# First layer of a four-layer graph network: out-of-block edge rows skipped in every tile's gather instead of in the last two tiles of a block

## The chip, the cores and the metric

The kernel runs on one core of one Trainium2 chip. A core has a matrix engine (PE in the profile, with its weight loads as PEld), three engines for elementwise work (DVE, ACT, POOL), a queue engine (SP) and 16 DMA engines that they share. The metric is the device time of one launch in microseconds. The time of the kernel before the change is the median of ten runs, 3303.32 us, the runs lying between 3298.07 and 3307.70 us.

## The reference, cut to what matters

Four layers follow each other, each added to its input. Only the first is touched:

```
edge_index = stack([src, dst])                  # 106250 edges, sorted by dst, 6250 nodes
def L0_gnn(x, edge_index, edge_attr, W1, b1, W2, b2):
    row, col = edge_index
    h = concatenate([x[row], edge_attr], axis=1)      # 256 + 256 wide
    h = relu(h @ W1 + b1)
    agg = segment_sum(h, col, 6250)
    cnt = segment_sum(ones, col, 6250)
    agg = agg / maximum(cnt, 1)
    return relu(concatenate([x, agg], axis=1) @ W2 + b2)
x = x + L0_gnn(layernorm(x), ...)
x = x + L0_ffn(...)        # attention over 131072 other edges, then 4 experts
x = x + L1_gnn(...)        # second sum over the 106250 edges
x = x + L1_ffn(...)        # gated experts
```

So each edge needs the row of its source node, already multiplied by the upper half of W1 (the kernel calls this table `y_dram`), plus its own attributes times the lower half of W1; the rectified sum is added up by destination node.

## The kernel before, in words

**Blocks and windows.** The 6250 nodes are cut into 49 blocks of 128 (the last has 106). As the edges are sorted by destination, a block's edges are contiguous. For each block the kernel takes a window of 2304 edges, 18 tiles (`CW`) of 128, that starts at the block's first edge; the start is counted on the chip (`start`, L1086) and clamped so that the window stays inside the edge list. With 17 edges per node a block has some 2176 edges, so in most blocks the edges of the next block lie in the last two tiles, numbers 16 and 17. In the last block the clamp moves the start back, and edges of the block before it lie in the first tiles.

**Source numbers.** `load_windows` (L1189) prepares seven blocks at a time: it reads source and destination numbers, turns them on PE, clamps them (L1219 to L1221), marks in `inside` which edges belong to the block (L1231, L1232), and writes `src1` (L1241), the row numbers for the gathers. In between, at L1236 to L1240, the tiles from `SKIP` on get special treatment: 8192 (`FAR`) is added to the number of each edge that is not inside, so that the number is beyond the table. In the first group of seven blocks the first block is left out (`int(b == 0)`).

**Gathers.** The first layer runs over 147 groups of six tiles, three groups for each block (`groups1`, `RUNS`: group 0 has tiles 0, 1, 7, 8, 14, 15, group 1 has 2, 3, 9, 10, 16, 17, group 2 has 4, 5, 6, 11, 12, 13). `load_sources(q)` (L1603) issues on POOL one indirect DMA for each tile of group q, each of which fetches 128 rows of 1 KB from `y_dram` into one of four ring buffers `h` (L1581). The call itself is in the helper `gather`, L1184. For a tile from `SKIP` on, of any block but the first, the gather is issued with a bounds check: a row number beyond 6249 is no error, and no row is fetched for it. What is left in the buffer from earlier use is multiplied by zero later.

**What a group does besides.** In the loop at L1741, one pass for each group, `hidden(q)` multiplies the group's edge attributes by W1 on PE into `ph` (24 matmuls of 256 columns, recorded at the helper line L1170), `turn` transposes the attributes of the next group on DVE (L1613), `join(q)` adds `ph` to the gathered rows on DVE (L1631) and rectifies on ACT (L1632), and `add_up(q)` sums over destinations by matmuls with a 0/1 matrix (L1650). Preparation of later windows and a sort for the second layer are fed in between in small steps. The order on each engine is the program's (`ordered.pin()`, L1769).

**What holds a gather back.** In pass q the gathers of group q+2 are issued, after `add_up(q-2)`. With four buffers, group q+2 uses the buffer of group q-2, so the first gather of a group waits for the PE's sums of the group four before it. What holds a join back is the slower of two: the group's matmuls in `ph` and its six gathers.

After the first layer come the attention of the second layer with its first experts (gathers `sg`, 1280 to 2160 us) and the second sum over edges (gathers `hg`, 2212 to 3250 us). Their gathers are issued without the check.

The lines that matter:

```
SKIP, FAR = CW - 2, 8192.0                                               # L945
far = g[:, int(b == 0) :, SKIP:]                                         # L1236
V.scalar_tensor_tensor(
    far, flat3(inside)[:, int(b == 0) :, SKIP:], -FAR, far, op0=OP.mult, op1=OP.add
)
V.tensor_scalar(far, far, FAR, None, op0=OP.add)                         # L1240
gather(rows_of(q)[:, j, 0:D], y_dram, idx, w > 0 and t >= SKIP)          # L1608
```

Of the kernel before, what the change touches and what calls it, by code (L numbers as in the profile page):

```python
# [918 lines left out]
def kernel(ctx: ExitStack, tc: tile.TileContext, a: dict, out: bass.AP):  # L919
# [22 lines left out]
    C2 = E2 // P  # L942
    assert E2 % P == 0
    CW = 18
    SKIP, FAR = CW - 2, 8192.0  # L945
    WE = CW * P
    G = 8

# [1905 lines left out]
```

## Time and profile before

| what | value |
|---|---|
| median of ten runs | 3303.32 us |
| the profiled execution's own time | 3305.04 us |
| its span in the profile | 3303.2 us |
| mean granted PE clock over the span | 0.895 of full speed |
| first layer's gathers: number, first and last start | 882, at 99.6 and 1242.5 us |
| busy time from 100 to 1250 us: PE, DVE, ACT, POOL | 1104.6, 912.1, 321.8, 859.2 us |
| DMA engines, mean busy share in that stretch | 0.89 |

The profile shows one execution. Busy time is counted from instruction to instruction for each engine; the short spell in which an engine starts its next instruction is not counted, which matters for POOL here: a gather is recorded with about 0.95 us and the next begins about 0.30 us after its end. The profiled execution took 1.7 us more than the median, and 1.8 us of its time lie outside the span.

### The profile page before, as it was taken

The page shows a single profiled execution, that of the slowest core. Times are in us where ns is not written, and L with a number is a line of the kernel's source. Part 1 is how long each engine was busy: PE and PEld are TensorE (multiplying, and loading weights), DVE is VectorE, ACT ScalarE, POOL GpSimd, SP SyncE. Part 2 cuts the span into 40 slices and gives each one's busy share as a digit, 9 for nine tenths or more (in the row PEclk, how much of TensorE's full clock was granted, in tenths as well). Part 3 has the DMA queues.
Part 4 walks back from the last instruction along what each step waited for, and adds up shares of the span by engine and source line. Part 5 has one row for each costly group of instructions (what it writes and reads, how often), then busy time and mean ns, then how long its engine had stood idle before and what let it go on. Part 6 is the DMA issues. An engine that isn't in the chain of part 4 may idle for free.

```text
span 3303.2 us, 59987 instructions
## 1 busy us (share of the span) xinstructions
PE 2996.2 (91%) x18517; PEld 2355.9 (71%) x18517; DVE 2186.1 (66%) x6516; ACT 1184.2 (36%) x2200; POOL 2277.1 (69%) x2720
## 2 busy tenths in 40 slices
PE   6899999999999989999999999956788888889997
PEld 5667777777777767888888888844566666656775
DVE  6678887788777766878686869862344444444464
ACT  5122222222222323556666668740112112112234
POOL 1677777777777774777776677427777777777772
PEclk9999999999999999999999999965577777777798
DMA  6889898989999873445454545532222222222221
GB/s 180 193 192 197 200 208 192 199 195 207 205 208 202 197 175 101 111 111 136 102 153 104 140 97 153 130 102 53 53 59 59 59 59 59 60 60 60 60 66 30
DMA packets 704935, 423.34 MB, mean 128 GB/s; under 512 B 538699, under 2 KB 647303, under 8 KB 704604
## 3 DMA queue, kind: packets, MB, share of 16 engines
q1 hardware_dynamic: 422972, 201.12, 23.5%
q0 software_dynamic: 88512, 171.58, 23.1%
q10 hardware_dynamic: 193120, 46.69, 7.0%
q8 instruction: 150, 2.46, 0.3%
q14 instruction: 181, 1.48, 0.2%
HBM read 382.75 MB, written 42.50 MB: 129 GB/s over the span
## 4 chain that ended last, share of the span: by engine, by line
PE 52%; POOL 16%; issue 10%; DMA 10%; DVE 7%; ACT 2%; SPq 2%; ACTq 0%; DVEq 0%; POOLq 0%
PE ph L1170 28%; POOL hg L1184 14%; PE py L1170 10%; PE pe L1650 4%; PE pt L1170 3%; DMA ea<-in_edge_attr_dram 3%; DMA hg<-hp_dram,src 3%; PE pe L2714 2%; DMA h<-y_dram,src 2%; DMA rb<-low_dram 1%; POOL h L1184 1%; PE po L2032 1%; POOL sg L1184 1%; DVE et L1613 1%; DVE E L2010 1%
## 5 line engine op out<-in xcount | busy, mean ns | idle before, releaser
L1184 POOL DMA_INDIRECT h<-y_dram,src x882 | 859.6, 975 | 366.9 <-issue 204.1
L1184 POOL DMA_INDIRECT hg<-hp_dram,src x831 | 785.5, 945 | 280.7 <-issue 239.5
L1170 PE MATMUL ph<-w1b,et 128*128 128x256 f32 x3528 | 830.9, 387 | 13.6 <-DVE et L1613 8.1
L1184 POOL DMA_INDIRECT sg<-gat_dram,src x612 | 612.0, 1000 | 270.1 <-issue 167.2
L1170 PEld LDWEIGHTS ph<-w1b,et 128*128 128x128 f32 x3528 | 658.7, 191 | 161.5 <-issue 74.9
L2714 PEld LDWEIGHTS pe<-eq,hg 128*128 128x128 f32 x2036 | 396.5, 259 | 300.4 <-issue 151.9
L2714 PE MATMUL pe<-eq,hg 128*128 128x96 f32 (+15 forms) x2036 | 452.1, 352 | 153.8 <-DMA hg<-hp_dram,src 134.9
L2691 DVE TENSOR_SCALAR eq<-px,dst,ew 128x96 f32<-128x96 f32 x831 | 262.2, 368 | 245.7 <-PE pe L2714 146.9
L1170 PE MATMUL py<-w,hh 128*128 128x256 f32 x1568 | 399.4, 393 | 13.2 <-ACT hh L1833 11.9
L1170 PE MATMUL ph<-b_all,w 128*128 128x256 f32 (+1 forms) x1600 | 402.1, 388 | 1.0 <-ACT hh L1833 1.0
L1632 ACT ACTIVATE h<-h 128x1536 f32<-128x1536 f32 x147 | 218.4, 1486 | 501.7 <-DMA ea<-in_edge_attr_dram 184.5
L1631 DVE TENSOR_TENSOR h<-ph,h 128x1536 f32<-128x1536 f32 x147 | 258.1, 1756 | 169.7 <-PE ph L1170 120.8
L1170 PEld LDWEIGHTS py<-w,hh 128*128 128x128 f32 x1568 | 282.1, 192 | 51.2 <-ACT hh L1833 17.0
L1170 PEld LDWEIGHTS ph<-b_all,w 128*128 128x128 f32 x1600 | 284.1, 192 | 30.9 <-ACT hh L1833 1.5
L1613 DVE STREAM_TRANSPOSE et<-ea 128x1536 f32<-128x1536 f32 x147 | 260.7, 1773 | 14.6 <-DMA ea<-in_edge_attr_dram 10.1
L1833 ACT ACTIVATE hh<-ph,b 128x256 f32<-128x256 f32 (+1 forms) x400 | 166.9, 466 | 125.4 <-PE ph L1170 105.7
L2010 DVE TENSOR_SCALAR E<-nodes,bits 128x256 bf16<-128x256 bf16 (+5 forms) x612 | 187.5, 345 | 36.3 <-PE po L2032 35.5
L1650 PE MATMUL pe<-h,eq 128*32 128x257 f32 x2496 | 181.2, 395 | 0.0
L1833 ACT ACT_TABLE_LOAD x102 | 130.9, 1283 | 24.3 <-PE ph L1170 14.3
L1165 ACT ACTIVATE b_all<-pt 128x256 f32<-128x256 f32 x147 | 54.1, 377 | 217.5 <-PE pt L1164 214.1
L1170 PE MATMUL py<-ew,g 65*128 65x256 f32 x392 | 126.0, 449 | 1.0 <-DVE miss L2799 1.0
L1650 PEld LDWEIGHTS pe<-h,eq 128*32 128x32 f32 x2496 | 72.7, 111 | 69.7 <-issue 34.1
(358 smaller groups left out, 3930.8 us busy)
## 6 DMA issues: line engine op xcount, KB each, us to landing
ea<-in_edge_attr_dram SPq DMA_DIRECT2D x784, 64.0 KB
ea<-in_edge_attr_dram ACTq DMA_DIRECT2D x392, 64.0 KB
w<-in_L_ffn_W_dram SPq DMA_DIRECT2D x48, 512.0 KB
y<-ys SPq DMA_DIRECT2D x96, 256.0 KB
rb<-low_dram SPq DMA_DIRECT2D x84, 256.0 KB
ea<-in_edge_attr_dram ACTq DMA_DIRECT2D x196, 96.0 KB
ea<-in_edge_attr_dram SPq DMA_DIRECT2D x196, 96.0 KB
h<-y_dram,src POOLq DMA_INDIRECT x882
```

Of the source, the lines that this page charges most:

```text
L1165: SC.activation(dst, pt.rearrange("p c k -> p (c k)"), AF.Copy)
L1170: TE.matmul(dst, lhs(c), rhs(c), start=c == 0, stop=c == n - 1)
L1184: GP.indirect_dma_start(out=dst, out_offset=None, in_=table[0:NP, :], in_offset=IndirectOffsetOnAxis(ap=idx, axis=0), **more,)
L1613: V.transpose(et[q].rearrange("p c m k -> p m c k"), ahead.pop(q).rearrange("p m (c k) -> p m c k", c=2),)
L1631: V.tensor_add(h, ph.pop(q), h)
L1632: SC.activation(h, h, AF.Relu)
L1650: TE.matmul(sums[w][b * Q : (b + 1) * Q, :], some[:, (b - lo) * Q : (b - lo + 1) * Q], rows_of(q)[:, j, 0:WS], start=(g, b, j) in begin, s ...
L1833: SC.activation(hidden[u][:, f, :n, :], ph[:, f - f0, :n, :], AF.Gelu, bias=b1[:, e, f : f + 1],)
L2010: V.tensor_scalar(Es[g, j][:, 0:n, :].rearrange("p b k -> p (b k)"), nodes16[:, 0 : n * P], bits.bitcast(F32)[:, g * G + j : g * G + j + 1 ...
L2032: TE.matmul(pos[g][bank][:, to * HP : (to + 1) * HP], E[:, b - b0, :], pays[g % 2][:, j, :], start=bank not in begun, stop=bank not in lat ...
L2691: V.tensor_scalar(equals[k][:, j, :], lanes[:, 0:NW], dst_of[:, t : t + 1], ew[:, t : t + 1], op0=OP.is_equal, op1=OP.mult,)
L2714: TE.matmul(sums[b][:, lo - t0 * P : hi - t0 * P], hg[:, j, :], eq[:, j, lo - n0 : hi - n0], start=False, stop=after >= (t0 + n) * P,)
```

## The change

One constant:

```
-    SKIP, FAR = CW - 2, 8192.0
+    SKIP, FAR = 0, 8192.0
```

Two things follow from it. At L1236 to L1240 the two operations on row numbers now go over all 18 tiles of a block (126 elements per partition for seven blocks, 108 in the first group) instead of two tiles (14 and 12 elements). And at L1608 every gather of blocks 1 to 48 is issued with the bounds check: 864 of 882 gathers instead of 96. In the built program this adds one register write on POOL for each such gather, 864 in place of 96. On PE, ACT and SP the instructions, their order and their waits are the same as before; on POOL only those register writes are new; on DVE the two operations are wider, and in the preparation of the first seven blocks a few small operations change places. No transfer, buffer or wait is added or taken away elsewhere. Which edges count is decided by `dst1` and the 0/1 matrix, as before.

## The prediction

> **What bounds the kernel now.** The page first, for the engines; then busy time by stretch, for the stage that the change touches; then POOL's timeline, the waits of that stage and the chain of waits.
>
> ```profile
> POOL 1677777777777774777776677427777777777772
> L1184 POOL DMA_INDIRECT h<-y_dram,src x882 | 859.6, 975 | 366.9 <-issue 204.1
> ```
>
> The changed gathers are one group: 882 of them, 975 ns each, all in slices 2 to 15 of 40. POOL's "7" looks like slack, but busy time leaves out the start of each instruction. The busy time by stretch says the same of the stage alone (columns: us, then busy us and count of PE, PEld, DVE, ACT, POOL, granted PE clock, DMA share, GB/s):
>
> ```profile
> 100.00:1250.00 1150.00, 1104.60 (x6817) 857.95 (x6818) 912.07 (x1864) 321.76 (x534) 859.21 (x882) 0.98 0.89 198
> ```
>
> PE is busy 96%, POOL only 75%. POOL's timeline (start, duration, engine, idle before it) corrects that:
>
> ```profile
> 133.53 0.95 POOL L1184 DMA_INDIRECT h<-y_dram,src  x1 [0.30 <-issue]
> 134.78 1.01 POOL L1184 DMA_INDIRECT h<-y_dram,src  x1 [0.30 <-issue]
> 136.10 1.00 POOL L1184 DMA_INDIRECT h<-y_dram,src  x1 [0.30 <-PE ph L1170]
> 137.41 0.96 POOL L1184 DMA_INDIRECT h<-y_dram,src  x1 [0.30 <-issue]
> 138.69 0.96 POOL L1184 DMA_INDIRECT h<-y_dram,src  x1 [0.31 <-issue]
> 139.95 0.95 POOL L1184 DMA_INDIRECT h<-y_dram,src  x1 [0.30 <-issue]
> ```
>
> A gather every 1.25 us, with 0.30 us of start-up between any two. 882 times 1.25 is 1103 us, against 1143.9 us from the first gather's start (99.6) to the last one's end (1243.4). Going through the timeline for gaps above 0.305 us, I find 18, which hold 15.5 us more than that; the rest is gathers that last somewhat longer than 0.947 us. So POOL too works almost without a pause. Who paces whom is in the waits and the chain:
>
> ```profile
> DVE h L1631 <- PE ph L1170: 118.0, 74, 8.5
> DVE h L1631 <- DMA h<-y_dram,src: 35.5, 13, 5.3
> ```
> ```profile
> 325.34 3.65 PE ph L1170 x16
> 332.49 3.65 PE ph L1170 x16
> ...
> 1108.81 3.84 DMA h<-y_dram,src
> 1114.07 3.71 DMA h<-y_dram,src
> ```
>
> The join (L1631) waited 74 times for the matmuls, 13 times for the gathers: early on PE sets the pace and POOL runs up to the ring's limit; later the chain runs through the gathers. By the timeline, group 24 starts gathering at 284.8, group 84 at 755.5, group 132 at 1124.4 us: 7.85 us a group in the first stretch, 7.69 in the second, where POOL had one gap, of 0.2 us. PE's matmuls of groups 84 and 132 start at 768.0 and 1126.6: PE then needs only 7.47 us a group. The two engines are a few per cent apart, so what is added to POOL cannot be hidden for long.
>
> **The change part by part.** *The check.* It is in the trace: 96 gathers have it, tiles 16 and 17 of blocks 1 to 48. In the lines above they are the 1.01 and the 1.00. Over all 96 the median is 1.008 us and the shortest 1.003; the gathers of tiles 0 to 3 and 6 to 15 have 0.947 at every place in the group, and the shortest 0.941. The start-up before them is 0.305 us in both. Does the price come from skipped rows? Counting edges in the reference's sorted list, 25 of the 96 have no edge outside the block: median 1.008. For 24 all 128 are outside: 1.0085. It is a price of the form, 61 ns, whatever is skipped. The two gathers after each checked pair (0.96, tiles 4 and 5) last 0.960, 13 ns longer than others; why, the trace does not say.
>
> Newly checked are 16 tiles in 48 blocks, 768 gathers: 768 x 61 ns = 46.8 us. If the 13 ns is paid on coming back to unchecked gathers, it goes, since there is nothing to come back to: 96 x 13 ns = 1.2 us less. Sum 45.6 us of POOL's time. Bounds, since no run of checked gathers longer than two is in the trace: 0.995 us if 13 ns of the price belongs to changing between forms (16 x 48 ns less 4 x 13 ns a block: 34.4 us), 1.021 if both add up in a long run (18 x 1.021 us against 17.19 us a block: 56.8 us). I take 1.008, the measured one. The checked gathers' mean is 1.035, so 27 ns above their median, where the others' is 20 above (0.967); 7 ns x 768 = 5.4 us more at most, and I take half.
>
> *The register writes.*
>
> ```profile
> L1184 POOLq MOVE  x96: 29/29/35, 127.5 to 1229.2; - x96
> ```
>
> 768 more of 29 ns would be 22.3 us if POOL's start-up grew by them. It does not: the start-up before checked gathers is 0.305 us like before others, the second of a pair too, whose write falls into it. Counted at nothing; without that cover 22.3 us more.
>
> *The rows saved.* In blocks 1 to 47 no tile below 16 holds an edge from outside. Only the last block does, whose window is pushed back: 128, 128, 128 and 97 rows in tiles 0 to 3, 481 rows of 1 KB. At the stage's 198 GB/s that is 2.5 us of transfer, at the end of a stage whose joins wait there for PE (1232 to 1254 us). Counted at nothing; 2.5 us would be the most. This is the gain that the change has, and it covers one block in 49.
>
> *The wider DVE operations.* L1237 lasted 173 ns and L1240 174 ns at 14 elements. The same forms at 126 elements, L1232 and L1221, last 291 and 227. So 171 ns for seven blocks, 1.2 us over the seven preparations. The first lies at 63 us, 36 us ahead of the first gather; the others are spread in a stage where DVE is busy 912 of 1150 us. Nothing; if each delayed a join, 1.2 us.
>
> *What of it reaches the end.* POOL gains 45.6 us of work but loses waiting: it had 15.5 us of gaps, where the ring was full because PE was late. A POOL that is slower meets them with the ring less full. I carried the new durations through the 147 groups, holding the kernel's two rules (a group starts after the sums of the group four before; a join after the matmuls as timed and 2.4 us after its last gather, which is what the tightest ones show), and delaying PE two groups later by what a join is late. Gaps left: 2.1 us. POOL then ends 45.6 - 15.5 + 2.1 = 32.2 us later, the last join 30.9 us later, since before it came 11 us after its gather and now 9.7. With 7 ns more a gather the last join moves by 35.9, so with half of it 33.4. By the paces: 45.6 us over 144 groups is 0.32 a group, so POOL needs 7.69 + 0.32 = 8.00, above PE's 7.85 and 7.47.
>
> What is late next: the order on PE is fixed, so experts of the second layer cannot fill PE's new pauses. The write of `gat_dram` at 1276 us hangs on the last block's sums, and the second layer's gathers on it (1279.7); PE is busy 913 of 960 us after that. Nothing there waits for a clock of its own, so I pass the shift on whole: 3303.2 + 33 = 3336 us of span, 3338 with the 1.8 us outside; against the median, 1.7 us below that execution, 3336.3. Forecast **3336 us**.
>
> **Two rules weighed.** The Trainium skill, "DMA: Bandwidth & Descriptors", section "Issuing engines are not separate DMA queues", says that the time to initiate a DMA is usually small beside the transfer. Here it is not: 1.25 us of POOL for 128 KB, which at 198 GB/s are 0.66 us. By the rule only the saved rows would count and the sum would be 3301 us; by the row it is 3336. The other speaks against the change: "TensorE: Matmul & The Clock Gate", section "HAM oscillation — how this bites in real kernels", wants no pause of PE above some 3.4 us, or its clock halves. The stage has seven stretches at half clock of 3.4 to 6.8 us between 105 and 1243 us and a granted mean of 0.98. I see pauses of half a microsecond a group coming, and by the rule add nothing; one more half-clock stretch of 6.8 us would cost PE 3.4 us, which it has to spare.
>
> **The rivals.** *PE goes on setting the pace; no change.* For it: 74 waits against 13, PE 96% busy. Against: the paces. It would hold only if a gather cost less than (7.85 - 7.69) / 6 = 27 ns more; the 96 rows show 61. Time 3301 to 3306. Chance 0.05, a little of it for a price that a long run of checked gathers does not pay. *Faster: changing between the forms is all that costs.* The place is POOL, the price the 96 x (61 + 13) ns = 7.1 us that it then no longer pays, decisive if a checked gather in a long run lasts 0.947 or less: at most 3303 - 7 = 3296, where POOL is the bound. Against it: the second of each pair costs as much as the first. Chance 0.02. *A smaller price, 0.995 us.* The same working gives 21 us: 3324. Chance 0.15. *A larger one:* 1.021 us with all of the 7 ns gives 46.5 us, 3350; and if the register writes showed too, up to 3372. Chance 0.13. *PE loses its clock in this stage as in the last, where it waits for gathers at a granted 0.73:* 1105 x 0.98 / 0.73 = 1483 us of PE work, over 300 us more. Against: PE would pause 7% of the time here, in short pieces. Chance 0.02. The forecast itself, 3329 to 3343, has 0.63.
>
> **Range and chances.** Leaving out the faster and unchanged cases and the far end, 3319 to 3352: from 5 us under the small price to 2 us over the larger. Within 0.2% (6.6 us) a measurement cannot tell from no change. Faster 0.02, same 0.05, slower 0.93.
>
> **What would show it.** The changed profile should have gathers `h` of about 1.01 us median in blocks 1 to 48, start-up still 0.30, last start near 1275 us; joins that wait more often for the gathers than for `ph`; PE's busy time in the stage unchanged and the stage longer; gathers `sg` and `hg` as before, shifted. I am wrong if the long run's median is 0.95, or the start-up grows by 29 ns, or POOL's gaps stay at 15 us, or the second layer takes up the delay.

## The result, and the profile after

The changed kernel takes 3324.9 us (median of 8 runs, 3322.95 to 3327.19); the kernel before, run beside it, 3302.46 us (median of 28). The ratio is 1.0068, with a 95% interval of 1.0059 to 1.0077: 22.4 us slower. The profiled execution took 3321.77 us, 3.1 us less than the median, and the one of before 2.6 us more than its median of 28; so the two spans differ by 16.8 us only (3320.0 against 3303.2), and stages are compared here rather than spans.

The page of the changed kernel, costliest groups (count | busy us, mean ns | idle before):

```profile
L1184 POOL DMA_INDIRECT h<-y_dram,src x882 | 896.9, 1017 | 353.1 <-issue 195.3
L1184 POOL DMA_INDIRECT hg<-hp_dram,src x831 | 784.9, 945 | 280.6 <-issue 238.3
```

The first layer's gathers have 37.3 us more busy time than before (859.6), and their mean rose from 975 to 1017 ns; the last stage's gathers `hg` have the mean that they had. POOL's timeline of the changed kernel, in the stretch shown of before (start, duration, engine, idle before it):

```profile
131.91 1.00 POOL L1184 DMA_INDIRECT h<-y_dram,src  x1 [0.30 <-issue]
133.21 1.00 POOL L1184 DMA_INDIRECT h<-y_dram,src  x1 [0.30 <-issue]
134.51 1.00 POOL L1184 DMA_INDIRECT h<-y_dram,src  x1 [0.30 <-issue]
135.82 0.99 POOL L1184 DMA_INDIRECT h<-y_dram,src  x1 [0.30 <-issue]
```

Before, two gathers of 18 were longer than the others; now all have the same 1.00 us, with the same start-up. The line view of the gathers in the first layer (count: shortest/median/longest ns, first and last start):

```profile
L1184 POOL DMA_INDIRECT h<-y_dram,src x882: 942/998/1458, 99.8 to 1267.0; - x177
```
```profile
L1184 POOLq MOVE  x864: 29/29/35, 114.3 to 1261.5; - x173
```

The median is 998 ns, not 947 and not 1008. The last gather starts at 1267.0 us instead of 1242.5. There are 768 more register writes, and the start-up has not moved. Busy time of the stage to 1270 us (PE, PEld, DVE, ACT, POOL, granted clock, DMA share, GB/s) and the join's waits (us, times, longest):

```profile
100.00:1270.00 1170.00, 1107.56 (x6799) 855.62 (x6800) 911.40 (x1862) 319.60 (x530) 896.70 (x882) 0.98 0.87 193
```
```profile
DVE h L1631 <- DMA h<-y_dram,src: 81.0, 32, 7.9
DVE h L1631 <- PE ph L1170: 79.2, 43, 8.4
```

PE has the work that it had (1107.6 us in a stretch 20 us longer, 1104.6 before) at the same granted clock. The join waited 32 times for gathers, 13 before, and 43 times for the matmuls, 74 before: POOL has taken over part of the pace. By the timeline, POOL's gaps beyond 0.305 us shrank from 15.8 to 2.9 us (every excess counted; the 15.5 us of the prediction are the 18 clear gaps alone). The first gather of the second layer starts at 1303.6 instead of 1279.7 us; from there to the end it is 2016 us, 2024 before, so nothing is lost later, and the other profiles below lie between 2012 and 2024 for that part whatever they do in the first layer, but for the kernels that change the last stage and the four runs with pauses told of below.

### The profile page after: what moved, and what is told of

Its sections match the earlier page's. It is cut to its first block, busy times and chain, and to the rows that moved or that the text cites. A ratio compares the mean times of both kernels' runs of the same rounds, so it can differ in the third digit from the quotient of the medians.

```text
span 3320.0 us, 60755 instructions
## 1 busy us (share of the span) xinstructions
PE 3003.3 (90%) x18517; PEld 2353.9 (71%) x18517; DVE 2183.2 (66%) x6516; ACT 1183.3 (36%) x2200; POOL 2313.4 (70%) x2720
## 3 DMA queue, kind: packets, MB, share of 16 engines
q0 software_dynamic: 88512, 171.09, 22.7%
## 4 chain that ended last, share of the span: by engine, by line
PE 47%; POOL 15%; DMA 14%; issue 11%; DVE 8%; SPq 2%; ACT 2%; ACTq 0%; DVEq 0%; POOLq 0%
PE ph L1170 24%; POOL hg L1184 12%; PE py L1170 10%; DMA ea<-in_edge_attr_dram 6%; PE pe L1650 3%; PE pe L2714 3%; PE pt L1170 3%; DMA hg<-hp_dram,src 3%; DVE et L1613 2%; DMA h<-y_dram,src 1%; POOL sg L1184 1%; PE po L2032 1%; POOL h L1184 1%; DMA rb<-low_dram 1%; DVE E L2010 1%
## 5 line engine op out<-in xcount | busy, mean ns | idle before, releaser
L1184 POOL DMA_INDIRECT h<-y_dram,src x882 | 896.9, 1017 | 353.1 <-issue 195.3
L1613 DVE STREAM_TRANSPOSE et<-ea 128x1536 f32<-128x1536 f32 x147 | 260.7, 1773 | 14.8 <-DMA ea<-in_edge_attr_dram 9.7
```

Of the source, the lines that this page charges most:

```text
L1184: GP.indirect_dma_start(out=dst, out_offset=None, in_=table[0:NP, :], in_offset=IndirectOffsetOnAxis(ap=idx, axis=0), **more,)
L1613: V.transpose(et[q].rearrange("p c m k -> p m c k"), ahead.pop(q).rearrange("p m (c k) -> p m c k", c=2),)
```

## The experiments

Theory F: a gather issued with the bounds check costs POOL a fixed time more, whatever it skips, and what of that exceeds POOL's gaps is in the time. Against it stood M (the marking, with skipped rows and wider DVE operations), D (the DMA engines as the bound) and P (another share of PE and POOL in the pace). Each time below is a median with the ratio to before in the same run.

**The check alone.** `e1_check_all`: the check on every gather of blocks 1 to 48, the marking as before.

```
-  gather(rows_of(q)[:, j, 0:D], y_dram, idx, w > 0 and t >= SKIP)
+  gather(rows_of(q)[:, j, 0:D], y_dram, idx, w > 0)
```

> Every gather of blocks 1 to 48 has the bounds check, but edges outside the block are marked only in tiles 16 and 17, as in the kernel before; so no further row is skipped and the DVE operations are as narrow as before. Theory F (the checked form itself costs POOL 51 ns a gather in a long run, whatever is skipped): gathers of 0.998 us at the median, last gather's end near 1267 us, time 22 us above before (3325). Theory M (the marking costs: skipped rows or wider DVE operations): gathers of 0.947 and 3303 us.

3321.16 us against 3298.70: ratio 1.0075 (1.0061 to 1.0089), 22.5 us. On its page the gathers' busy time is the changed kernel's but for 0.9 us:

```profile
L1184 POOL DMA_INDIRECT h<-y_dram,src x882 | 896.0, 1016 | 350.1 <-issue 193.4
```

The gathers' median is 998 ns at nearly every place in the block, the last one ends at 1264.2 us. The check alone, without a row more skipped or an element more on DVE, gives the whole change.

**The marking alone.** `e2_mark_all`: every tile is marked, the check stays in tiles 16 and 17, and in block 48, where the 481 other rows lie.

```
-  SKIP, FAR = CW - 2, 8192.0
+  SKIP, FAR = 0, 8192.0
-  gather(..., w > 0 and t >= SKIP)
+  gather(..., w == T - 1 or (w > 0 and t >= CW - 2))
```

> The other half alone: all 18 tiles are marked, as in the changed kernel, but the check is on in tiles 16 and 17 of blocks 1 to 47 and in all tiles of block 48, the only one where marked rows lie elsewhere. The same rows are skipped as in the changed kernel. Theory F: 16 more checked gathers, 0.8 us of POOL, which the gaps swallow: within 2 us of before. Theory M: the changed kernel's time, 3325 us.

3296.37 us against 3298.70: 0.9995 (0.9986 to 1.0003). The same line of this kernel is that of before, with 1.6 us more:

```profile
L1184 POOL DMA_INDIRECT h<-y_dram,src x882 | 861.2, 976 | 363.0 <-issue 206.2
```

The same rows are skipped as in the changed kernel and nothing is lost or measurably won. M is out.

**Runs of two, three and four.** `e3_from_tile9`:

```
-  SKIP, FAR = CW - 2, 8192.0
+  SKIP, FAR = 9, 8192.0
```

> SKIP = 9: nine tiles a block are checked, in runs of two, four and three, with unchecked ones between. If the first two gathers of a run cost 10 ns more than later ones and the two unchecked ones after it 13 ns (theory F with a price for changing form), durations are 1.008 twice, then 0.998, then 0.960 twice, then 0.947; POOL has 21.5 us more work, and carried through the groups with the ring's rule the last join moves 10 us: 3312 to 3314. Without a price for changing form: 0.998 and 0.947 throughout, 14.9 us of work, last join 5.5 us later: 3308. If the time followed POOL's work one for one, with no gaps to take some of it: 3324.

3308.12 us against 3298.70: 1.0034 (1.0022 to 1.0045), 9.4 us. POOL's timeline of this kernel, tiles 0, 1, 7, 8 and 14 of one block:

```profile
310.72 0.96 POOL L1184 DMA_INDIRECT h<-y_dram,src  x1 [0.30 <-issue]
311.98 0.96 POOL L1184 DMA_INDIRECT h<-y_dram,src  x1 [0.30 <-issue]
313.24 0.95 POOL L1184 DMA_INDIRECT h<-y_dram,src  x1 [0.30 <-issue]
314.49 0.94 POOL L1184 DMA_INDIRECT h<-y_dram,src  x1 [0.30 <-issue]
315.74 1.01 POOL L1184 DMA_INDIRECT h<-y_dram,src  x1 [0.30 <-issue]
```

Two unchecked gathers after a checked run at 0.96, two at 0.95 and 0.94, then the first of the next run at 1.01. The medians over blocks 1 to 48, tile by tile in the order of issue (ns, the checked ones starred):

```
tile   0   1   7   8   14*   15*   2   3   9*    10*   16*  17*   4   5   6   11*   12*   13*
ns   960 960 947 947  1008  1008 960 960 1008  1009  999  999  960 960 947  1008  1008  999
```

The first two of a run cost 61 ns more, the third and fourth 51 to 52, and the two gathers after a run 13. Durations and time both fit the price with a change of form: gathers take 19.5 us more in all (21.5 expected), of which 9.4 reached the end (10 expected), because POOL's gaps fell to 3.2 us. The time alone would leave the decision thin: the rival without such a price, at 5.5 us, lies just below the interval of 7.3 to 14.8. The durations exclude it.

**No check at all.** `e4_no_check`: marking and check taken out, all 882 gathers fetch all rows.

```
-  far = g[:, int(b == 0) :, SKIP:]
-  V.scalar_tensor_tensor(far, ...)
-  V.tensor_scalar(far, far, FAR, None, op0=OP.add)
-  gather(..., w > 0 and t >= SKIP)
+  gather(...)
```

> No check and no marking in any tile: all 882 gathers fetch all their rows, 6165 rows (6.3 MB) more than the kernel before. Theory F: POOL has 7.1 us less work; where PE sets the pace this only lengthens POOL's gaps, so 0 to 5 us faster, 3298 to 3303. Rival D (the DMA engines, busy 0.89 of the stage, are as much a bound): 6.3 MB at 198 GB/s are 32 us of transfer, and the time rises, by up to that.

3299.02 us against 3298.70: 1.0003 (0.9993 to 1.0013). The gathers' busy time falls by 11.9 us (7.1 expected), POOL's gaps grow from 15.8 to 20.3, the DMA share from 0.89 to 0.92. The stage by the same view as in the prediction:

```profile
100.00:1250.00 1150.00, 1107.27 (x6845) 862.67 (x6846) 913.82 (x1857) 321.55 (x534) 847.70 (x882) 0.99 0.92 204
```

The number of rows above was too high: the queue of the gathers moved 6.15 MB more than before, which is 6030 rows (the 135 of the first block, which is never checked, had been counted in), or 31 us at 198 GB/s. In its profile the second layer's first gather comes 7.0 us sooner after the first layer's than before, yet the median does not show it. These 31 us of transfers are not in the time, so D as a bound is out; whether the 0.03 of DMA share took back a few us that POOL gave is open.

**POOL relieved far.** `e5_no_tile17`: the kernel before without one gather in each of 48 blocks.

```
+  if w > 0 and t == CW - 1:
+      continue
```

> The kernel before without the gathers of tile 17 in blocks 1 to 48 (their edges are summed with whatever row the buffer held, so that part of the first layer is left out). POOL has 48 x (1.008 + 0.305) = 63 us less work. If the kernel before is paced by PE for most of the first layer (theory F), little comes of it: 0 to 10 us, 3289 to 3299, and POOL's gaps grow to some 75 us. If POOL paces it (rival P), most of it comes: 3240 to 3255.

3285.11 us against 3298.27: 0.9958 (0.9943 to 0.9972), 13.2 us less, for 63 us less on POOL. The join's waits in this kernel:

```profile
DVE h L1633 <- PE ph L1170: 146.2, 92, 6.9
DVE h L1633 <- DMA h<-y_dram,src: 8.2, 3, 4.8
```

92 waits for matmuls, 3 for gathers, and 64 us of gaps on POOL (some 75 expected): this is PE's own pace. It is 13 us below the kernel before, 3 us more than I had allowed: the kernel before already lost that to POOL.

The durations in this kernel do not repeat the pattern of e3. The checked gather, now alone in its block, lasts 1011 ns at the median, but the two after it 945 and 947; instead the third after it (tile 6) lasts 957 and tile 14 of the next block 961. A pause of POOL ahead of them, which 41 of the 48 have, does not explain it: the seven without one last 947, and in the kernel before ten gathers of tile 4 come after a pause and last 958 all the same. Why is open.

**POOL loaded further.** `e6_one_more`: the changed kernel with a gather more in each of 48 blocks.

```
+  spare = wy.tile([P, D], F32, name="spare")
   gather(rows_of(q)[:, j, 0:D], y_dram, idx, w > 0 and t >= SKIP)
+  if w > 0 and t == 8:
+      gather(spare, y_dram, idx, True)
```

> The changed kernel with one more checked gather in each of blocks 1 to 48 (tile 8 a second time, into a buffer that nobody reads). POOL has 48 x (0.998 + 0.305) = 62.5 us more work, the DMA engines 6.3 MB more. If the changed kernel is paced by POOL through nearly the whole layer (theory F: only 2.9 us of gaps are left), all but some 3 us of it reaches the end: 3321 + 60 = 3381. If PE still paced half of it (rival P): 3350.

3374.11 us against 3298.27: 1.0231 (1.0214 to 1.0248), 75.8 us; that is 53.4 more than the changed kernel's 22.4, of 62.5 us put on POOL. Its waits:

```profile
DVE h L1634 <- DMA h<-y_dram,src: 134.1, 53, 8.0
DVE h L1634 <- PE ph L1170: 53.1, 24, 8.0
```

The gathers now end more of the join's waits than anything else does, and POOL has no gap left. Most of the load arrives, 7 us less than theory F expected and 24 more than rival P did, among other things because the layer's last matmuls of `ph` now start 5.7 us after the last gather's end where they started 9.6 us after it.

**The same price in other stages.** The check on the gathers `hg` of the last stage (`e7_check_hg`, again as `e9_check_hg2` and `e12_check_hg3`) and on `sg` of the second layer (`e8_check_sg`, again as `e10_check_sg2`), the first layer being as before; and the changed kernel once more (`e11_change_again`).

```
-  gather(gathered[k][:, j, :], hp_dram, src_of[:, t : t + 1])
+  gather(gathered[k][:, j, :], hp_dram, src_of[:, t : t + 1], True)
```
```
-  gather(got[g][:, j, :], gat_dram, src2[:, g * G + j : g * G + j + 1])
+  gather(got[g][:, j, :], gat_dram, src2[:, g * G + j : g * G + j + 1], True)
```

> The kernel before with the bounds check on the 831 gathers hg of the last stage instead (512-byte rows; every number is within the table, so no row is skipped); the first layer is as before. POOL there runs from 2212.3 to 3250.6 us with no gap beyond the start-up of 0.305 us. Theory F: 0.996 us a gather, 831 x 51 ns = 42 us, all of it in the time: 3340. Rival H (a checked form costs nothing where nothing is skipped or the rows are short): 3298.

> The kernel before with the bounds check on the 612 gathers sg of the second layer, whose POOL stretch of 878 us holds 80 us of gaps beyond the start-up. Theory F: the same 51 ns each, 31 us of POOL's time, but the gaps take most of it: 0 to 6 us, 3298 to 3304, and the gaps fall to some 50 us. If the price always reached the end: 3329.

> The same kernel as in the run before with hg checked, because in that run every kernel, the one before too, had pauses of POOL, PE and DVE that no other run has (before: 4190 us). Where before is back at 3298 to 3303: theory F 42 us more, 3340 to 3345; rival H no change.

> The same kernel as in the run before with sg checked, for the same reason. Theory F: 31 us of POOL's time, most of it in gaps, 0 to 6 us in all; if the price always reached the end 31 us.

> The changed kernel itself once more. If before takes about 3300 us in this run: 22 us above it. If before again takes some 4200 us, with 285 us of gaps on POOL in the first layer and PE waiting too: theory F says that POOL has room for its 37 us there, so within 10 us of before, while gathers still last 0.998 and the gaps shrink by about what the gathers gain; a price that reaches the end whatever paces the layer would show 22 us or more.

> The kernel with hg checked. If before takes about 3300 us in this run, theory F expects 42 us above it (POOL has no gaps in that stage there), rival H nothing. If before takes some 4200 us, the 160 us of gaps that POOL then has in that stage take the price: within 10 us.

In the four runs from e7 to e10 every kernel, the one before too, took about 4200 us, with pauses of all engines that no other run has. Their pages put 12 to 16% of the chain that ended last down to "another core or an unknown queue", which stands on no other page here. They ran on two chips (e7 and e8 on one, e9 and e10 on the other), the other experiments on three others; the cause stayed open. Ratios are to the kernel before in the same condition.

```
run                  this us   before us   ratio (95% interval)
e7_check_hg          4195.42   4189.91     1.0013 (0.9986 to 1.0039)
e9_check_hg2         4261.13   4258.20     1.0025 (0.9996 to 1.0054)
e8_check_sg          4166.27   4189.91     0.9945 (0.9922 to 0.9967)
e10_check_sg2        4223.19   4258.20     0.9933 (0.9905 to 0.9961)
e12_check_hg3        3341.14   3299.89     1.0119 (1.0104 to 1.0135)
e11_change_again     3323.39   3299.89     1.0071 (1.0057 to 1.0084)
```

The line view of `hg` in the kernel before and in e12, both without those pauses:

```profile
L1184 POOL DMA_INDIRECT hg<-hp_dram,src x831: 940/945/1666, 2212.3 to 3249.7; - x167
L1184 POOL DMA_INDIRECT hg<-hp_dram,src x831: 992/998/1615, 2208.2 to 3290.3; - x167
```

With rows of 512 bytes and nothing to skip, a gather goes from 945 to 998 ns, the gathers' busy time rises by 44.5 us and the time by 41.2; 42 were expected from 831 x 51 ns. There POOL had no gap to take any of it. In e7 and e9, where POOL had 159 us of gaps in that stage by the timeline of e7, the gathers lasted 1000 ns just the same and the time did not move measurably (at most 16 and 23 us by the intervals). The same price is thus paid in full where POOL has no gaps, and hidden at least in good part where it has them. On `sg` the gathers went from 946 to 997 ns, and no loss showed; but the kernel was 24 to 35 us faster than before in both runs, which no theory here expects. By the profiles the gain lies in that stage itself: from its first gather to the first `hg` it takes 1293 and 1337 us, against 1332 and 1370 in e7 and e9. I have no cause for that, and it was measured only among those pauses. The changed kernel once more (e11) is 23.5 us slower than before, 22 expected.

## Why the prediction was right, and where it was off

**The price is of the form, not of the rows: shown.** e1 has the check without the rows and is 22.5 us slower; e2 has the rows without the check and is not. In the changed kernel too, tiles with no row outside and tiles with 128 have the same 998 ns. What POOL does in the 51 ns no run shows.

**The size of the price: this term was mis-sized.** The forecast, 3336 us, was 11 us too high, and the result lies below the 3329 to 3343 that I thought most likely, though inside the range of 3319 to 3352. I took 1.008 us for a gather in a long run, the value of the pairs; it is 0.998. The 13 ns on the gathers after a pair, which I noted and could not explain, belong, by e3, to a cost for changing form, of which the rest sat in the pairs' own 1.008; the trace of before, with no run longer than two, could not separate it. That reading is not complete, since the lone checked gathers of e5 show another pattern. With 0.998 the sum is 768 x 51 ns less 96 x 10 ns (the old pairs become cheaper) less 96 x 13 ns, 37.0 us instead of 45.6; the profile has 37.3. Carried through the groups as in the prediction, this moves the last join by 22.5 us instead of 30.9: 8.4 of the 11 us. The lower bound of my range of prices, 0.995, was near this, and the rival with the smaller price, at 3324 us, came within 1 us of the result.

**The 7 ns for disturbance: wrong.** I added half of 5.4 us because checked gathers had lain further above their median. In the changed kernel the mean of all gathers is 19 ns above the median, against 20 for the unchecked ones before. The term should have been nothing; it is the other 2.5 of the 11 us.

**What the gaps take: right.** I expected 2.1 us of gaps to remain of 15.5; counted in the same way, 2.6 remain. The carrying through the groups was done again after the result, with 0.998 and a join 2.1 us after its last gather; it gives the 22.5 us (22.8 with the 2.4 us of the prediction). The time moved by 22.4, the last join of the profile by 23.7. The kernels with other loads on POOL fit one picture: the busy time of the gathers, with 0.305 us for each one added or left out, against the time:

```
kernel          POOL work, us   time, us
e5_no_tile17        -62.8        -13.2
e4_no_check         -11.9         +0.3
e2_mark_all          +1.6         -2.3  (within its interval of no change)
e3_from_tile9       +19.5         +9.4
e1_check_all        +36.4        +22.5
changed kernel      +37.3        +22.4
e6_one_more         +99.7        +75.8
```

A fifth of POOL's work reaches the end below the kernel before, half of it up to e3, three quarters from e3 to the changed kernel, six sevenths beyond. The kernel before sits in the bend of this curve. My rival of an unchanged time had the right observation, 74 waits against 13, but counted waits do not tell how near the other engine is.

**What was counted at nothing.** The register writes: the start-up is 0.305 us before and after, and in e1, so counting them at nothing was right. The reason that I gave, that a write falls into the start-up of its gather, was not. Taken in the order of the program, each of the 96 writes of before ends at least 1.4 us before its gather starts (5.8 us at the median, some five gathers ahead), and 70 of them run while an earlier gather is still running. These earlier gathers last no longer for it: 947 ns with a write inside or without in the kernel before, 998 either way in the changed one.

The DVE operations, in the line view of the changed kernel:

```profile
L1237 DVE SCALAR_TENSOR_TENSOR ix_g<-inside,ix_g x7: 272/291/292, 62.0 to 786.9; 128x126 f32<-128x126 f32 x6, 128x108 f32<-128x108 f32 x1
L1240 DVE TENSOR_SCALAR ix_g<-ix_g x7: 219/228/230, 62.3 to 787.2; 128x126 f32<-128x126 f32 x6, 128x108 f32<-128x108 f32 x1
```

291 and 228 ns at the median, where the neighbours of that width had promised 291 and 227; e2 has them and loses nothing. The rows saved won nothing that e2 could measure.

PE's clock in the stage is 0.98 as before. PE's idle time there grew from 45.4 to 62.4 us, but five of its pauses are longer than 3.4 us before and five after, the longest 5.8 and 5.6 us. Half-clock stretches that start after 105 us are six before (my seventh is one of 10.2 us that ends at 105) and seven after. The rule of the Trainium skill on pauses of PE ("TensorE: Matmul & The Clock Gate", section "HAM oscillation — how this bites in real kernels") fits these traces in part: a half-clock stretch starts in or within 5 us after four of the five long pauses before and all five after, and two stretches in each have no such pause ahead of them. The change did not put it to the test, since it added no long pause. The rule on initiating a DMA ("DMA: Bandwidth & Descriptors", section "Issuing engines are not separate DMA queues") would have had 3301 us. Here POOL spends 1.25 us on each gather before and 1.30 after, start-up included, and the measurement, 3324.9, decides against applying it.

**The shift passed on whole: right.** The second layer's first gather came 23.9 us later in the profile, the last stage's 17.2, within the spread of the stage between; the medians differ by 22.4.

**Signs that I named and that did not come.** I expected joins to wait more often for gathers than for matmuls; it is 32 against 43, in e11 39 against 41, and only in e1 41 against 35. In time waited the two are even (81.0 and 79.2 us). The last gather starts at 1267.0 us, not near 1275, as each gather costs less than I took. The two engines share the pace; POOL does not hold it alone until e6.

## What to carry to other kernels

Read an engine that issues gathers from start to start: here 0.95 us of busy time came with 0.30 us of start-up, and an engine shown at 75% had 15.8 us of gaps in 1144. Before extending an option from a few instructions to all, take its price from those few, ask whether it depends on what the option saves, and count where that saving lies: here it lay in two tiles of 18 and one block of 49, and the price in every gather. Where two engines pace a stage within a few per cent, neither adding nor removing work on one of them moves the time one for one; load it both ways to see where you stand.

## What the runs showed of the hardware that was not expected

Changing between checked and unchecked gathers has a cost of its own. In e3, with runs of two to four, the first two checked ones last 1008 ns instead of 998 and the first two unchecked ones after a run 960 instead of 947; with one checked gather alone, in e5, it lasts 1011 ns and the two after it show nothing.

A gather's time on POOL did not depend on how many of its 128 rows were skipped, nor on the size of a row (947, 946 and 945 ns for rows of 1024, 96 and 512 bytes). What skipping saves is time of the DMA engines. The queue that carries all gathers has 88,512 packets in the kernel before, in the changed one and in e4 alike; only the bytes differ (171.58, 171.09 and 177.73 MB). In the first layer of the kernel before, a packet of four rows has 4096 bytes and takes 233 ns at the median; with all four rows skipped it has 16 bytes and takes 11. The layer's packets on this queue take 449 us on the average of the 16 engines before and 472 in e4. So the saving falls where e4 found no bound, and the price on POOL, which shares the pace.

The kernel, changed or not, took some 4200 us instead of 3300 in the four runs from e7 to e10, with the same durations of gathers, transposes and matmuls at the median and only more pauses between them; what caused these was not found.
